# Image 2's sorted products by half steps, and its adding gathers without free steps

## The chip, the cores and the metric

The kernel runs on one core of a Trainium2 chip. The metric is the device time of one launch in microseconds (us). The engines of the core run programs of their own and wait for each other by semaphores: TensorE (PE: matmuls and transposes), ScalarE (ACT: activations, evictions of PSUM), VectorE (DVE: elementwise work and reductions), GpSimd (POOL: here powers, and the issue of indirect DMAs) and SyncE (SP: issues DMAs). ACT issues a few DMAs too.

## The reference

Two layers on four images x of 32 channels and 128 x 128 pixels, all in float32:

```python
# layer 0: attention over the 4096 pixels of each image, by 2 x 2 pixel groups as 128 channels
energy = einsum('bci,bcj->bij', q, q);  d = sqrt(diagonal(energy))
attn = softmax(energy / (d[:, :, None] * d[:, None, :]))
out = gamma * einsum('bcj,bij->bci', q, attn) + xs
# layer 1, on the result as tokens t of 128 features
t = t + L1_attn(layernorm(t), Wk, Wq, Wv)      # linear attention, 8 heads
t = t + L1_ffn(layernorm(t), router_w, ...)    # top 2 of 8 experts per token
```

The expert part computes `softmax(x @ router_w + router_b)`, takes the two largest of eight probabilities per token, scales them to a sum of one, and adds the two experts' products with these weights.

## The kernel before

**Layer 0** (`attend`). An image's 4096 pixels are 8 chunks of 512. The matrix of energies is symmetric, so only chunk pairs (i, jc) with jc up to i are computed, in blocks of 128 x 512. A *step* does one block: PE computes `pe` (L551), ACT takes its exp with a row sum (L554), PE multiplies the block of two steps before into `po` (L440), VectorE transposes it in groups (L369), SP moves groups through DRAM and back (L473 and L488), and some five steps later PE multiplies the mirrored block into `pg` (L375), while ACT sums it once more (`junk`, L380). An image takes 144 steps; the last one (image 3) takes 152, since in its last chunk row two blocks are computed a second time the other way round (`pe_back`, L529 and L532).

**Layer 1** (`layer1`) follows an image's attention. `close_rows(kc)`, kc = 0 to 3, finishes eight row groups: it divides by the sums (L704), adds (L726), takes statistics (L729) and their power on POOL (`rsa`, L164 called from L632, then `nba`, L633), normalises on ACT (L639; for kc = 2 and 3 of the last image half of it on VectorE, L739) and adds the Gram matrix on PE (L671). `close_rows` waits until the transposed shares that its rows need have been added. Then come the small matrices, the linear attention, and the router.

The experts of images 0 to 2 work on sorted tokens, by two halves h of an image (`sorted_experts`, L915). 32 *scatters* of POOL (L994) write the normalised tokens to DRAM in the order of their expert. Then a loop (L1070) goes over 39 tiles of 128 sorted tokens, as 20 pairs: it loads pair `at` (L1022, on SP), evicts what the step before left in PSUM (`done()`: ACT copies transposed tiles, L1032; VectorE scales products by the token's weight, L1038; SP stores them to DRAM, L1042), and issues on PE the products of pair `at - 4` (L1056) and the transposes of pair `at - 3` (L1063). So a pair's transposes are evicted one iteration later and are the weights of the matmuls after that. At last 32 *adding gathers* of POOL (L1107) bring each token's two results back from DRAM and add them to the token in `acc`. They go by groups of eight; ACT fetches the group's tokens first (L1092), and SP stores the finished group to the output (L1098). Image 3's experts are done without sorting, in `last_parts`.

**What sets the order.** For PE, VectorE, ACT and SP the program order is the order of issue (`manual_schedule`, L1315), and POOL's powers, first scatters and gathers are pinned too. The order comes from generators: each `yield` ends one advance. `attend` yields before and after each step, and the main loop (L1333 to L1349) moves the streams at both places, so a step moves a stream of layer 1 by two advances; `idle(n)` is 2n yields, that is n steps. Image 2's stream therefore runs along image 3's attention. Within a stream the parts run side by side (`stagger`, L166). Each scatter and gather waits for the last exp that was issued before it, "not more of these at a time than steps have". A half's gathers begin when its loop has ended and the other half's scatters (for h = 0) or gathers (for h = 1) are issued. What is left of the streams when image 3's attention ends is issued at once (L1357 to L1359: the drain), in the order of the images, before `last_parts`.

The variable `rate` (L1101) is the number of gathers between two yields: 1 for images 0 and 1, 2 for image 2, whose groups moreover had one free step after each four gathers.

Of the kernel before, what the change touches and what calls it, by code (L numbers as in the profile page):

```python
# [22 lines left out]
def kernel(  # L23
# [45 lines left out]
    B, C, H, W = x.shape  # L69
# [59 lines left out]
    def wait_for(inst, others, why):  # L129
        for other in others:  # L130
            tc.add_manual_dep(
                inst, other.name, mybir.DependencyInfo(mybir.DependencyClass.Sync, mybir.DependencyReason.DATA),
                reason=why,
            )
# [24 lines left out]
    def pinned(inst):  # L159
        tc.keep_in_program_order(inst)  # L160
        return inst
# [16 lines left out]
    def idle(n):  # L178
        for _ in range(2 * n):
            yield  # L180
# [416 lines left out]
    def layer1(b, st):  # L597
# [276 lines left out]
        def attention_rows(u):  # L874
# [32 lines left out]
            if u % 2:  # L907
                for _ in route(u // 2):
                    yield
                    yield  # L910
                yield
                yield
                yield from sorted_experts(u // 2)

        def sorted_experts(h):  # L915
# [66 lines left out]
            def offset(ap):  # L982
                return bass.IndirectOffsetOnAxis(ap=ap, axis=0)
# [4 lines left out]
            for n in range(2 * HR):  # L988
# [19 lines left out]
                if n % 4 == 3 and (b < B - 2 or n % 8 == 7):  # L1008
                    yield from idle(1)
            turns[h].append("moved")  # L1010
            xs_made[h][:], xs_read[h][:] = scatters, []
            yield from idle(3)

# [7 lines left out]
            def load(g, n):  # L1021
                inst = nc.sync.dma_start(bufs[g % 6][:, :n], rows_of(xs[h], g, n))  # L1022
                wait_for(inst.ins, xs_made[h], "a tile holds tokens of any row")
                xs_read[h].append(inst.ins)
# [45 lines left out]
            for at in range(len(pairs) + 5):  # L1070
                if at < len(pairs):
                    load(*pairs[at])
                if done:
                    done()
                yield
                turned, applied = (pairs[at - d] if 0 <= at - d < len(pairs) else None for d in (3, 4))
                done = products(turned, applied) if turned or applied else None
                yield
# [11 lines left out]
            def fetch(g):  # L1090
                accs[g] = work.tile([P, 4, D], F32, tag="acc", name=f"acc_{b}_{g}", bufs=3)
                nc.scalar.dma_start(accs[g], t2[:, ts(g, 4)])  # L1092

            def put(g):
                for r1 in range(2):
                    for s in range(2):
                        p0 = s * 64 + r1 * 32
                        nc.sync.dma_start(dst_out[s, r1, :, ts(g, 4), :], accs[g][p0 : p0 + 32])  # L1098

            groups = list(range(r0 // 4, (r0 + HR) // 4))  # L1100
            rate = 1 if b < B - 2 else 2  # L1101
            fetch(groups[0])
            yield from idle(2)
            for g in groups:
                for n in range(8):
                    i, k = n // 4, 4 * g + n % 4
                    inst = nc.gpsimd.indirect_dma_start(  # L1107
                        accs[g][:, n % 4, :], None, ys, offset(place[:, i, k : k + 1]), compute_op=ALU.add
                    )
                    wait_for(pinned(inst).ins, exps, "not more of these at a time than steps have")  # L1110
                    if (n + 1) % rate == 0:
                        yield
                        yield
                    if rate == 2 and n % 4 == 3:
                        yield from idle(1)
                    if n == 3 and g != groups[0]:
                        put(g - 1)
                    if n == 3 and g != groups[-1]:
                        fetch(g + 1)
# [280 lines left out]
```

## Time and profile before

| | us |
|---|---|
| median of the runs (3) | 1706.38 |
| lowest to highest | 1706.34 to 1708.11 |
| the profiled execution | 1708.0 |
| its span, first to last instruction | 1706.2 |
| mean granted clock of TensorE | 0.989 |

| engine | busy us | share of the span |
|---|---|---|
| PE | 1645.4 | 96% |
| ACT | 927.5 | 54% |
| VectorE | 880.4 | 52% |
| POOL | 630.9 | 37% |

The profile is of one execution. A row of a timeline gives start, duration, engine, line of the code, operation, what is written and read, how often, and in brackets how long the engine sat idle before and what ended that. The chain of waits goes back from the last instruction, at each point to what released it. Busy PE is modelled, so full PE is not PE at its peak. Image 3's attention runs from about 1156 to 1566 us; `last_parts` ends the kernel.

### The profile page before, as it was taken

The numbers are of one execution on the slowest core, as the hardware profiler recorded it, in microseconds if no ns is written. First come the engines' busy times: TensorE is split into PE (matmuls) and PEld (weight loads), VectorE is DVE, ScalarE is ACT, GpSimd is POOL, SyncE is SP. The second block draws the span as 40 slices with busy tenths as digits, with TensorE's granted clock in tenths as the row PEclk, the third lists the DMA queues.
The fourth block names the chain that finished last, engine by engine and source line by source line (L and its number), as shares of the span: only waits on it lengthen the run. The fifth ranks groups of instructions, "written<-read, shape, count | busy, mean of one in ns | idle before, by whom it ended". The sixth has DMA issues, their size and how long they took to land.

```text
span 1706.2 us, 21751 instructions
## 1 busy us (share of the span) xinstructions
PE 1645.4 (96%) x5458; PEld 876.4 (51%) x5458; DVE 880.4 (52%) x2251; ACT 927.5 (54%) x2893; POOL 630.9 (37%) x565
## 2 busy tenths in 40 slices
PE   8999999999999999999999999999999999999288
PEld 5444544455554455555554455555554455546243
DVE  4433334467485334377477334357568333346187
ACT  3555445466565555556575555556565555555076
POOL 1000000011024432454554532455555640567666
PEclk9999999999999999999999999999999999999699
DMA  4554756754458687985678676895578867993201
GB/s 133 169 178 155 208 177 212 254 178 162 164 162 261 209 248 214 250 229 148 185 216 255 229 223 215 249 251 159 166 210 240 260 213 229 236 248 63 44 12 39
DMA packets 248555, 326.53 MB, mean 191 GB/s; under 512 B 31472, under 2 KB 180080, under 8 KB 234096
## 3 DMA queue, kind: packets, MB, share of 16 engines
q1 hardware_dynamic: 206416, 285.62, 52.9%
q0 software_dynamic: 33792, 25.58, 8.5%
q10 hardware_dynamic: 8224, 13.93, 2.7%
q8 instruction: 46, 0.75, 0.2%
q14 instruction: 77, 0.63, 0.1%
HBM read 154.49 MB, written 175.80 MB: 194 GB/s over the span
## 4 chain that ended last, share of the span: by engine, by line
PE 81%; DVE 7%; ACT 4%; POOL 3%; DMA 2%; issue 2%; SPq 1%; ACTq 0%; DVEq 0%; POOLq 0%
PE po L440 23%; PE pe L551 22%; PE pg L375 19%; PE pys L1056 3%; PE py L1192 2%; PE pg L396 2%; POOL acc L1107 2%; PE pys L1063 1%; ACT xn L639 1%; PE pgram L671 1%; PE pat L797 1%; DVE df L704 1%; PE ptq L313 1%; ACT pr L554 1%; DVE F L369 1%
## 5 line engine op out<-in xcount | busy, mean ns | idle before, releaser
L554 ACT ACTIVATE pr<-pe 128x512 f32<-128x512 f32 (+1 forms) x576 | 322.3, 560 | 517.0 <-PE pe L551 429.9
L440 PE MATMUL po<-pr,qT 128*128 128x512 f32 (+3 forms) x1152 | 549.8, 559 | 3.9 <-ACT o L445 2.7
L551 PE MATMUL pe<-qn,qn 128*128 128x512 f32 x896 | 458.9, 594 | 2.0 <-ACT pr L554 1.7
L375 PE MATMUL pg<-F,qT 128*128 128x512 f32 x880 | 449.6, 592 | 0.8 <-DVE F L369 0.6
L1107 POOL DMA_INDIRECT acc<-ys,place x192 | 301.9, 1572 | 304.7 <-ACT pr L554 198.3
L369 DVE STREAM_TRANSPOSE F<-pr 128x512 f32<-128x512 f32 x440 | 306.4, 702 | 165.7 <-ACT pr L554 129.9
L440 PEld LDWEIGHTS po<-pr,qT 128*128 128x128 f32 x1152 | 214.8, 190 | 250.7 <-issue 222.2
L380 ACT ACTIVATE junk<-F 128x512 bf16<-128x512 f32 x440 | 272.8, 620 | 1.0 <-DMA F<-blocks 1.0
L375 PEld LDWEIGHTS pg<-F,qT 128*128 128x128 f32 x880 | 166.8, 190 | 195.2 <-issue 179.0
L994 POOL DMA_INDIRECT xs<-xn,place x192 | 185.6, 967 | 196.7 <-ACT pr L554 123.6
L551 PEld LDWEIGHTS pe<-qn,qn 128*128 128x128 f32 x896 | 152.6, 191 | 100.5 <-issue 93.3
L385 DVE TENSOR_TENSOR o<-o,pg 128x512 f32<-128x512 f32 x110 | 75.5, 686 | 214.3 <-PE pg L375 207.2
L1038 DVE TENSOR_TENSOR results<-pys,xn 128x256 f32<-128x256 f32 x120 | 50.1, 417 | 190.6 <-ACT xn L1032 151.7
L164 POOL TENSOR_TENSOR rn<-ss,neg_half 128x8 f32<-128x8 f32 (+1 forms) x17 | 26.9, 1582 | 321.2 <-DVE ss L325 321.2
L554 ACT ACTIVATION_READ_ACCUMULATOR pr<-pe 128x1 f32 x576 | 111.9, 194 | 0.0
L1032 ACT ACTIVATE xn<-pys 128x256 f32<-128x256 f32 x120 | 45.2, 377 | 114.9 <-PE pys L1063 95.7
L1056 PEld LDWEIGHTS pys<-ew_sb,xn 128*128 128x128 f32 x468 | 70.0, 191 | 48.4 <-issue 46.8
L551 PE MATMUL pe<-qn 128*128 128x512 f32 (+3 forms) x256 | 90.2, 435 | 0.7 <-ACT qn L344 0.7
L380 ACT ACTIVATION_READ_ACCUMULATOR junk<-F 128x1 f32 x440 | 84.4, 192 | 0.0
L639 ACT ACTIVATE xn<-T,nba,rsa 128x128 f32<-128x128 f32 x120 | 49.2, 483 | 43.5 <-POOL nba L633 43.5
L1056 PE MATMUL pys<-ew_sb,xn 128*128 x468 | 71.6, 275 | 0.0
L164 POOL TENSOR_TENSOR rsa<-dm_a,neg_half 128x8 f32<-128x8 f32 x16 | 30.1, 1881 | 112.0 <-DVE sv_a L631 111.7
(211 smaller groups left out, 1506.5 us busy)
## 6 DMA issues: line engine op xcount, KB each, us to landing
blocks<-F SPq DMA_DIRECT2D x110, 1024.0 KB
F<-blocks SPq DMA_DIRECT2D x220, 192.0 KB
F<-blocks SPq DMA_DIRECT2D x220, 128.0 KB
xn<-xs SPq DMA_DIRECT2D x114, 132.0 KB
ys<-results SPq DMA_DIRECT2D x114, 128.0 KB
F<-blocks SPq DMA_DIRECT2D x220, 64.0 KB
below<-F SPq DMA_DIRECT2D x31, 384.0 KB
out_dram<-acc SPq DMA_DIRECT2D x128, 64.0 KB
```

The costliest lines, as they stand in the source:

```text
L164: pinned(nc.gpsimd.tensor_tensor(dst, src, neg_half.to_broadcast(list(src.shape)), ALU.pow))
L369: f()
L375: nc.tensor.matmul(pg.rearrange("p (a f) -> p a f", a=4), st["qT"][i][:, ib, :], G[:, :, ib], start=(ib == 0), stop=(ib == NJ - 1),)
L380: nc.scalar.activation(junk, G[:, :, ib], AF.Copy, accum_out=st["sums"][:, NJ * i + ib, jc : jc + 1])
L385: nc.vector.tensor_tensor(o, o, pg.rearrange("p (a j c) -> p a j c", a=4, c=S), ALU.add)
L440: nc.tensor.matmul(row["po"][:, lo:hi], qT[blk // NJ][:, blk % NJ, :], w, start=start, stop=(row["left"] == 0))
L551: nc.tensor.matmul(pe[:, c0:], qn[jc][:, ts(j, P)], qn[i][:, c0:], start=True, stop=True)
L554: nc.scalar.activation(pr[:, c0:], pe[:, c0:], AF.Exp, accum_out=sums[:, t, i : i + 1]).ins
L639: nc.scalar.activation(xn[:, k, :D], T[:, k, :], AF.Identity, scale=rs[:, k, :], bias=nb[:, k, :])
L994: inst = nc.gpsimd.indirect_dma_start(xs[h], offset(place[:, i, k : k + 1]), xn[:, k, :], None)
L1056: nc.tensor.matmul(p[:, 2 * P + j * D : 2 * P + j * D + D], bufs[6 + g % 2][:, j, :D], weights[:, bass.ds(begins[2 * (g % 2) + j], D)], st ...
L1107: inst = nc.gpsimd.indirect_dma_start(accs[g][:, n % 4, :], None, ys, offset(place[:, i, k : k + 1]), compute_op=ALU.add)
```

## The change

It concerns image 2 (`b == B - 2`) alone and has two parts. In the loop of `sorted_experts` the yield between the evictions and the products goes, so that an iteration takes one advance, half a step, where it took two. And among the adding gathers the free step after each four goes, so that two are issued with every step. Loads, stores, products, evictions, gathers and their number stay as they are, and so do images 0, 1 and 3.

```diff
@@ -1008,6 +1008,7 @@
                 if n % 4 == 3 and (b < B - 2 or n % 8 == 7):
                     yield from idle(1)
             turns[h].append("moved")
+            hurried = b == B - 2
             xs_made[h][:], xs_read[h][:] = scatters, []
             yield from idle(3)
 
@@ -1072,7 +1073,8 @@
                     load(*pairs[at])
                 if done:
                     done()
-                yield
+                if not hurried:
+                    yield
                 turned, applied = (pairs[at - d] if 0 <= at - d < len(pairs) else None for d in (3, 4))
                 done = products(turned, applied) if turned or applied else None
                 yield
@@ -1111,8 +1113,6 @@
                     if (n + 1) % rate == 0:
                         yield
                         yield
-                    if rate == 2 and n % 4 == 3:
-                        yield from idle(1)
                     if n == 3 and g != groups[0]:
                         put(g - 1)
                     if n == 3 and g != groups[-1]:
```

## The prediction

> **What bounds the kernel now.** I read the page first, then the chain of waits of the last 170 us, then timelines by engine and the busy times by stretch. Times below are microseconds from the span's start.
>
> ```profile
> span 1706.2 us, 21751 instructions
> PE 1645.4 (96%) x5458; PEld 876.4 (51%) x5458; DVE 880.4 (52%) x2251; ACT 927.5 (54%) x2893; POOL 630.9 (37%) x565
> PE 81%; DVE 7%; ACT 4%; POOL 3%; DMA 2%; issue 2%; SPq 1%; ACTq 0%; DVEq 0%; POOLq 0%
> ```
>
> TensorE sets the time nearly everywhere. The busy times by stretch (length, then PE, PE loads, DVE, ACT, POOL busy with counts, granted clock, DMA share, GB/s) show where it doesn't:
>
> ```profile
> 1460.00:1500.00 40.00, 40.00 (x153) 22.89 (x152) 15.58 (x29) 21.34 (x65) 23.69 (x17) 1.00 0.95 241
> 1580.00:1609.00 29.00, 0.00 (x0) 0.00 (x0) 0.00 (x0) 0.00 (x0) 24.64 (x17) 0.57 0.38 54
> ```
>
> From 1580 to 1609 only GpSimd (POOL) works. The timelines of VectorE, POOL and ScalarE (ACT) say on what (start, duration, engine, line, operation; in brackets the idle time before and what ended it):
>
> ```profile
> 1578.90 0.17 DVE L631 TENSOR_SCALAR sv_a<-sv_a 128x8 f32<-128x8 f32 x1
> ...
> 1605.45 1.54 POOL L1107 DMA_INDIRECT acc<-ys,place  x1 [0.30 <-issue]
> 1606.43 2.27 POOL L164 TENSOR_TENSOR rsa<-dm_a,neg_half 128x8 f32<-128x8 f32 x1
> 1608.78 0.20 POOL L633 TENSOR_TENSOR nba<-sv_a,rsa 128x8 f32<-128x8 f32 x1
> 1609.02 1.65 ACT L639 ACTIVATE xn<-T,nba,rsa 128x128 f32<-128x128 f32 x4 [33.27 <-POOL nba L633]
> ```
>
> The chain of waits goes the same way, from these gathers to rsa, nba, ACT and then PE:
>
> ```profile
> 1606.99 1.72 POOL rsa L164
> ...
> 1609.02 0.50 ACT xn L639
> ...
> 1609.57 3.79 PE pgram L671 x16
> ```
>
> Image 3's last row statistics (kc = 3) are ready at 1579.07, but their power (rsa) stands on POOL behind image 2's last 18 gathers, which the program put there when the stream was drained. Free of them, nba would be done at 1579.07 + 0.04 + 1.67 + 0.08 + 0.20 = 1581.0 (1.67 is rsa alone, at 1567.11) instead of 1608.98. The prize is **28.0 us**.
>
> [...]
>
> **Where the change puts things.** I count image 3's attention steps 1 to 152 (one exp of L554 or L532 each). Nearly every step moves image 2's stream by two advances, one yield each, one before and one after the step; between one step's second advance and the next step's first no attention work is issued. That order matters below.
>
> Half 0's sorted products (L1070 to L1080) take 25 yields instead of 50, from step 79. Its gathers also need half 1's scatters, which end in step 99 as before; fetch and idle(2) put the first gather in step 102 instead of 110. A group of 8 gathers takes 4 steps instead of 6 (the removed idle(1) comes twice a group). So half 0 gathers in steps 102 to 119, half 1 in 122 to 138 (before: 139 and on, 18 left for the drain). All are issued 14 steps before attention ends. The 28.0 us go, and with them the cold clock after the idle: the 16 matmuls of pgram took 3.79 us against 2.40 at 1568.88, and the first pgv some 0.3 more: **1.7 us**.
>
> **Cost 1: two products back to back.** Before, a step with a pair takes 3.24 us, without 2.58 (exps at 1501.56, 1504.80; 1510.73, 1513.30): a product costs 0.66, PE never waiting. The number of products is unchanged, so these 0.66 only move. But a product's matmuls need the tile that ScalarE evicted from the product before (L1032), and now two products often stand next to each other:
>
> ```profile
> 1503.52 0.38 PE L1063 MATMUL pys<-ident,xn 128*128 128x128 f32 x2
> 1503.94 0.38 ACT L1032 ACTIVATE xn<-pys 128x256 f32<-128x256 f32 x1 [1.08 <-PE pys L1063]
> 1504.35 0.42 DVE L1038 TENSOR_TENSOR results<-pys,xn 128x256 f32<-128x256 f32 x1 [2.73 <-ACT xn L1032]
> ```
>
> From the start of the last transpose (1503.63) to the eviction 0.31, eviction 0.38, to the next matmul 0.05 (ACT ends 1574.41, PE goes on 1574.46), less the 0.11 at which they follow anyway: 0.63. [...] between 0 and 0.25 I take 0.1: 0.73. Counting the yields along the steps, 8 products of each half are such a second one: 16 x 0.73 = 11.7. The other 24 follow a step, but their eviction now stands on ACT behind that step's exp and junk: exp start + 0.58 + 0.62 + 0.38 + 0.05 = 1.63, where the product's matmul came at 1.51 and its weight load at 1.09. Between 0 and 0.5 I take 0.22: 5.3. **Sum 17** (13 to 21). PE is the bound there (40.00 of 40.00 busy), so nothing hides it.
>
> **Cost 2: gathers now queue before an earlier rsa.** Back to back a gather takes 1.84:
>
> ```profile
> 1505.75 1.54 POOL L1107 DMA_INDIRECT acc<-ys,place  x1 [2.43 <-ACT pr L554]
> 1507.60 1.54 POOL L1107 DMA_INDIRECT acc<-ys,place  x1 [0.30 <-issue]
> 1509.44 1.54 POOL L1107 DMA_INDIRECT acc<-ys,place  x1 [0.30 <-ACT junk L380]
> ```
>
> Two a step are 3.68 us against 2.58 of a step without products. Half 0's gathers lie mostly beside half 1's products (2.58 + 2 x 0.66 + 0.95 = 4.85 us a step) and POOL keeps up; half 1's don't. Image 3's first rows (kc = 0) issue their rsa in step 137, unchanged (it waits for the transposed shares, not for "sorted"), now behind 30 gathers. From step 122's exp (1487.30 before): 0.95 to the first gather, 29 x 1.84 + 1.54 = 54.9, 2.03 from the last gather to ACT's normalise (1606.99 to 1609.02), 1.64 for it, 0.27 for pgram's last row: 59.8. PE gets past that pgram (L671, after step 140) at 1539.32 - 1487.30 = 52.0, less 4 for six products no longer there: 48.0.
>
> ```profile
> 1535.54 1.64 ACT L639 ACTIVATE xn<-T,nba,rsa 128x128 f32<-128x128 f32 x4
> 1537.08 0.58 ACT L554 ACTIVATE pr<-pe 128x512 f32<-128x512 f32 x1
> 1538.43 1.05 PE L671 MATMUL pgram<-xn 128*128 128x128 f32 x8
> ```
>
> Behind the waiting normalise stand exps of steps 140 and on; behind pgram all PE. **11.8 us** (10 to 14). After that PE's clock is halved as at 1609; there 0.11 of 31 us were lost, 3.4, of which 0.7 in a dip from 1638.7 on: **2.6 us** (1 to 4).
>
> **What is moved at no or little cost.** Each pair's load and store (SP, 132 and 128 KB) come twice a step, 4 issues of 0.42; with the block moves 2.5 us of SP in 4.85. A load follows the store of two products before; two steps and five products later its transposes come, at the least 2 x 2.58 + 4.4 x 0.66 + 3 x 0.73 + 2 x 0.22 = 10.7 us, against 1.4 to evict and issue and the 2.7 to 5.9 that transfers in the chain of waits took to land. DMA: 241 GB/s x 3.24 us is 781 KB a step; 260 and 43 KB for the gathers more make 1084 KB in 4.85 us, 224 GB/s, no denser than now. Stores of gathered groups (L1098) stand on SP before image 3's last block moves, and wait for late gathers: group 5's are landed 32 us after step 122's exp, the move of step 134 is then at 34 instead of 32; its shares come after the pgram stall, which covers 2 us. ACT's fetches reuse a buffer stored 4 steps before. For all this **1 us** (0 to 4); without its cover a late load stops PE one for one.
>
> **Sum against the profiled execution** (1708.0, its span 1706.2, 1.8 outside): -28.0 - 1.7 + 17 + 11.8 + 2.6 + 1 = +2.7, so 1710.7. The median of the runs is 1.6 lower: 1709.1.
>
> **Rivals.** *A, the above*: the 28 us are handed back, 1709 (own range 1702 to 1718). *B, faster*: TensorE waits less than I think between two adjacent products, at L1056 after L1032. For it speaks that the modelled matmul ends are no measurement; against, ACT's 0.38 alone times 16 is 6. If all adjacent products cost 4 together: -29.7 + 4 + 15.4 = -10, 1696. The sign turns where they cost 14.3 in all, and 0.2% is reached below 11. *C, slower*: loads land late. SP is in order; a burst of six block moves takes 2.8 us, and a semaphore shared with an ACT fetch held SP up to 5.4 (its wait list). Some 6 bursts in the doubled loops at 2 us each: 12 more, 1721. Against: 10.7 - 1.4 - 5.9 leaves 3.4 us to spare after the slowest landing. *D, it does not do what it says*: half 0's gathers still wait for late stores and part of the drain stays, with Cost 1 paid: 1720. Against: the stores end in step 93.
>
> **Chances.** A 0.55, B 0.20, C 0.18, D 0.07. No change within 0.2% (3.4 us) is about what measurement tells. A gives 0.05 faster, 0.22 same, 0.28 slower; B 0.16 and 0.04; C and D slower: 0.21, 0.26, 0.53. Range 1695 to 1721: it leaves out the far halves of B, C and D.
>
> **What would show it.** Right: no POOL gather after some 1575; kc = 3's rsa starts at DVE's end; steps of 4.5 to 5 us with PE idle before L1056; a PE idle of 10 to 14 us before the first pgram of image 3, with ACT L639 waiting for nba, and the clock at half after it. Wrong: PE busy throughout the doubled loops (B), PE waiting at L1063 for DMA (C), or gathers up to kc = 3's rsa (D).

## The result, and the profile after

| | before | after |
|---|---|---|
| median of 7 runs each, us | 1706.38 | 1713.20 |
| lowest to highest | 1705.69 to 1708.40 | 1711.24 to 1715.61 |
| ratio, 95% interval | | 1.0038 (1.0026 to 1.0049) |
| profiled execution, its span | 1708.0, 1706.2 | 1711.8, 1710.0 |

The changed kernel is slower by 0.38%. Between the profiled executions the difference is 3.8 us, between the medians 6.8: the profiled one of before lay 1.6 over its median, that of after 1.4 under. What follows accounts for the 3.8. In the changed file L1032, L1056, L1063 and L1107 are L1033, L1057, L1064 and L1109.

The page of after, its head and its engines:

```profile
span 1710.0 us, 21761 instructions
...
PE 1654.2 (97%) x5458; PEld 874.0 (51%) x5458; DVE 878.9 (51%) x2251; ACT 926.2 (54%) x2893; POOL 628.7 (37%) x565
```

PE is busy 8.8 us more with the same 5458 instructions. Busy times of after by stretch (length, then PE, PE loads, DVE, ACT, POOL busy with counts, clock, DMA share, GB/s):

```profile
1382.00:1420.00 38.00, 33.09 (x136) 18.14 (x135) 12.37 (x25) 16.22 (x50) 10.65 (x12) 1.00 0.61 180
1449.00:1497.00 48.00, 42.49 (x176) 23.94 (x175) 15.00 (x34) 20.05 (x64) 30.66 (x20) 1.00 1.02 254
...
1555.00:1572.00 17.00, 5.21 (x15) 2.59 (x14) 0.00 (x0) 2.79 (x9) 14.29 (x11) 0.77 0.45 76
```

The first two stretches lie in half 0's and half 1's products, where PE now idles 4.91 and 5.51 us; the third is a new stall, in which POOL alone works. The waits of after, TensorE's (waited for in all, times, longest), name both:

```profile
PE pgram L671 <- ACT xn L639: 13.9, 4, 11.8
PE pys L1057 <- ACT xn L1033: 10.2, 17, 1.3
```

**The products.** Two adjacent ones in the timeline of after:

```profile
1400.84 0.38 PE L1064 MATMUL pys<-ident,xn 128*128 128x128 f32 x2
1401.31 0.38 ACT L1033 ACTIVATE xn<-pys 128x256 f32<-128x256 f32 x1 [1.08 <-PE pys L1064]
...
1401.75 0.52 PEld L1057 LDWEIGHTS pys<-ew_sb,xn 128*128 128x128 f32 x4 [0.77 <-ACT xn L1033]
1401.75 0.71 PE L1057 MATMUL pys<-ew_sb,xn 128*128 x4 [0.53 <-ACT xn L1033]
```

The transposes, their eviction by ACT and the next product's matmuls follow one after the other. A doubled step takes 4.91 us (exps at 1403.58 and 1408.49) where 2.58 + 2 x 0.66 would be 3.90. The exp of step 130 comes 20.5 us later than before.

**The gathers.** POOL's timeline of after around the stall and at the end of attention:

```profile
1566.82 1.54 POOL L1109 DMA_INDIRECT acc<-ys,place  x1 [0.30 <-issue]
1567.81 2.26 POOL L164 TENSOR_TENSOR rsa<-dm_a,neg_half 128x8 f32<-128x8 f32 x1
1570.15 0.20 POOL L633 TENSOR_TENSOR nba<-sv_a,rsa 128x8 f32<-128x8 f32 x1
...
1613.26 1.63 POOL L164 TENSOR_TENSOR rsa<-dm_a,neg_half 128x8 f32<-128x8 f32 x1 [9.96 <-DVE sv_a L631]
```

The last row is kc = 3's power: it starts as VectorE ends, no gather before it. The second is kc = 0's: it ends a row of 30 gathers begun at 1512.90, and ACT and PE stood behind it (ACT's and PE's timelines of after):

```profile
1570.39 1.65 ACT L639 ACTIVATE xn<-T,nba,rsa 128x128 f32<-128x128 f32 x4 [14.21 <-POOL nba L633]
```

```profile
1570.93 2.08 PE L671 MATMUL pgram<-xn 128*128 128x128 f32 x8 [11.79 <-ACT xn L639]
```

The clock was recorded at half from 1564.17 to 1574.41, and these 8 matmuls took 2.08 us, where the next 8 took 1.05. From the exp of step 139 to that of step 142 another 13.7 us are lost (14.3 by step 140, of which 0.6 come back). So: -28.0 (kc = 3's power no longer queued) + 20.5 + 13.7 - 2.4 (warm clock at the end: the 16 matmuls of pgram 2.07 us in place of 3.79, the first pgv 2.10 in place of 2.59, the rest small) = +3.8.

### The profile page after: what moved, and what is told of

It is laid out like the page before. It is cut to its first block, busy times and chain, and to the rows that moved or that the text cites. A ratio compares the mean times of both kernels' runs of the same rounds, so it can differ in the third digit from the quotient of the medians.

```text
span 1710.0 us, 21761 instructions
## 1 busy us (share of the span) xinstructions
PE 1654.2 (97%) x5458; PEld 874.0 (51%) x5458; DVE 878.9 (51%) x2251; ACT 926.2 (54%) x2893; POOL 628.7 (37%) x565
## 5 line engine op out<-in xcount | busy, mean ns | idle before, releaser
L440 PE MATMUL po<-pr,qT 128*128 128x512 f32 (+3 forms) x1152 | 549.6, 559 | 3.9 <-ACT o L445 2.0
L551 PE MATMUL pe<-qn,qn 128*128 128x512 f32 x896 | 458.7, 594 | 2.0 <-ACT pr L554 1.7
L1109 POOL DMA_INDIRECT acc<-ys,place x192 | 300.2, 1564 | 265.7 <-ACT pr L554 193.7
L440 PEld LDWEIGHTS po<-pr,qT 128*128 128x128 f32 x1152 | 214.7, 190 | 251.5 <-issue 224.4
L551 PEld LDWEIGHTS pe<-qn,qn 128*128 128x128 f32 x896 | 153.7, 191 | 107.4 <-issue 99.9
L1057 PEld LDWEIGHTS pys<-ew_sb,xn 128*128 128x128 f32 x468 | 67.0, 191 | 63.6 <-issue 32.9
L1033 ACT ACTIVATE xn<-pys 128x256 f32<-128x256 f32 x120 | 45.1, 376 | 96.7 <-PE pys L1064 83.8
L551 PE MATMUL pe<-qn 128*128 128x512 f32 (+3 forms) x256 | 91.0, 438 | 0.7 <-ACT qn L344 0.7
L1057 PE MATMUL pys<-ew_sb,xn 128*128 x468 | 75.5, 283 | 11.8 <-ACT xn L1033 10.2
L1192 PE MATMUL py<-ew_sb,xn 128*128 128x512 f32 x128 | 61.3, 621 | 5.3 <-ACT tmp L1149 4.1
```

What stands on the lines that cost most here:

```text
L440: nc.tensor.matmul(row["po"][:, lo:hi], qT[blk // NJ][:, blk % NJ, :], w, start=start, stop=(row["left"] == 0))
L551: nc.tensor.matmul(pe[:, c0:], qn[jc][:, ts(j, P)], qn[i][:, c0:], start=True, stop=True)
L1057: nc.tensor.matmul(p[:, 2 * P + j * D : 2 * P + j * D + D], bufs[6 + g % 2][:, j, :D], weights[:, bass.ds(begins[2 * (g % 2) + j], D)], st ...
L1109: inst = nc.gpsimd.indirect_dma_start(accs[g][:, n % 4, :], None, ys, offset(place[:, i, k : k + 1]), compute_op=ALU.add)
L1192: nc.tensor.matmul(bank, xn[:, k, :D], ew_sb[:, 4 * h : 4 * h + 4, :], start=True, stop=True)
```

## The experiments

Theory T: the products lose their time in the round trip from PE to ACT and back between adjacent products; the second loss is the queue of gathers ahead of kc = 0's power. Its rivals: R1, the products' loops lose their time to the transfers, twice as many a step; R2, the gathers are the whole loss; R3, the stall is of something else than the gathers; R4, at twice the pace the transfers are the limit wherever the products stand; R5, half 1's gathers must start by step 122 to be out of the way; R6, after the attention POOL has room for the gathers, so that the order in the drain alone gives the 28 us. *Delay* is how much later than before the exp of step 130 comes, less the offset that step 78 had already; *stall* what is lost from there to step 142; *left* the gathers that POOL starts after the last exp; *power* is the start of kc = 3's power.

| kernel | delay | stall | left | power | median us | ratio to before (95%) |
|---|---|---|---|---|---|---|
| before | | | 20 | 1606.43 | 1706 to 1708 | |
| after | 20.6 | 13.7 | 0 | 1613.26 | 1713.20 | 1.0038 (1.0026 to 1.0049) |
| half steps alone | 20.5 | 0 | 9 | 1607.04 | 1707.06 | 1.0000 (0.9991 to 1.0008) |
| gathers alone | 0.7 | 7.1 | 5 | 1597.42 | 1695.96 | 0.9932 (0.9915 to 0.9948) |
| tile used later | 14.4 | 14.6 | 0 | 1609.15 | 1707.50 | 1.0000 (0.9991 to 1.0009) |
| free steps in half 1 | 20.3 | 0 | 0 | 1600.64 | 1698.02 | 0.9943 (0.9926 to 0.9959) |
| transposes ahead | 17.4 | 14.6 | 0 | 1610.98 | 1712.90 | 1.0041 (1.0026 to 1.0056) |
| the two above together | 19.5 | 0 | 0 | 1598.85 | 1697.69 | 0.9945 (0.9931 to 0.9959) |
| half steps in half 1 | 10.0 | 1.5 | 10 | 1600.20 | 1700.25 | 0.9957 (0.9943 to 0.9971) |
| in half 1's last ten iterations | 10.4 | 0 | 9 | 1596.63 | 1696.36 | 0.9937 (0.9924 to 0.9951) |
| before, power first | 0 | 0 | 20 | 1579.46 | 1696.30 | 0.9935 (0.9921 to 0.9948) |
| last ten, power first | 11.4 | 0 | 9 | 1593.19 | 1689.96 | 0.9896 (0.9881 to 0.9911) |

**Each part of the change alone.** The first keeps the free steps among the gathers, the second keeps the whole steps of the products. Against the changed kernel:

```diff
+                    if rate == 2 and n % 4 == 3:
+                        yield from idle(1)
```

```diff
-                if not hurried:
-                    yield
+                yield
```

> Half steps alone: image 2's products take half a step per pair as in the changed kernel, the gathers keep the free step after each four. Theory T (TensorE waits for the eviction between two adjacent products; the gathers' queue is the second loss): the exp of step 130 comes 20.5 us (18 to 23) after that of before, as in the changed kernel. Half 1's gathers then go in steps 128 to 151, some 10 of them ahead of the power of kc = 0, at POOL's pace: TensorE's idle time before image 3's first pgram is under 4 us (11.8 in the changed kernel). About 8 gathers are left when attention ends, kc = 3's nba comes at about 1607 (1608.98 before), in all 1704 (1700 to 1709). Rival R2 (the products cost nothing worth naming, the whole loss is that of the gathers on POOL): the exp of step 130 comes less than 5 us late, and the time is about 1690.

> Gathers without free steps alone, the products stay at a step per pair. T: no delay in the products' loops (exp of step 130 within 1.5 us of before). Half 0's gathers end some 8 steps earlier, half 1's go in steps 133 to 151. Some 8 gathers stand ahead of kc = 0's power: TensorE idles 0 to 4 us before image 3's first pgram. POOL falls some 10 us behind by the end of attention, so kc = 3's nba comes at 1590 to 1595 (1608.98 before): 1690 (1685 to 1696). R2 (the gathers back to back are the whole loss): slower than before, 1712 or more.

The 20.5 us go with the half steps and the stall with the gathers: R2 falls. POOL's timeline with half steps alone shows why the first brings nothing: kc = 0's power finds a short queue, but kc = 3's has the rest of the gathers ahead of it.

```profile
1552.56 1.54 POOL L1109 DMA_INDIRECT acc<-ys,place  x1 [0.30 <-issue]
1553.93 1.88 POOL L164 TENSOR_TENSOR rsa<-dm_a,neg_half 128x8 f32<-128x8 f32 x1
...
1606.04 1.54 POOL L1109 DMA_INDIRECT acc<-ys,place  x1 [0.30 <-issue]
1607.04 2.26 POOL L164 TENSOR_TENSOR rsa<-dm_a,neg_half 128x8 f32<-128x8 f32 x1
```

With the gathers alone the time fell by 11 us, not by the 16 expected: kc = 0's power came at 1541.36, still behind back-to-back gathers, and so did kc = 1's and 2's later. PE waited 4.5, 3.1 and 5.1 us for the three. POOL's timeline and TensorE's wait list of that kernel:

```profile
1540.37 1.54 POOL L1107 DMA_INDIRECT acc<-ys,place  x1 [0.30 <-issue]
1541.36 2.26 POOL L164 TENSOR_TENSOR rsa<-dm_a,neg_half 128x8 f32<-128x8 f32 x1
```

```profile
PE pgram L671 <- ACT xn L639: 15.0, 7, 5.1
```

**The round trip taken away.** A product uses the tile turned two iterations before.

```diff
-            for at in range(len(pairs) + 5):
+            for at in range(len(pairs) + 5 + hurried):
+                if done:
+                    done()
                 if at < len(pairs):
                     load(*pairs[at])
-                if done:
-                    done()
...
-                turned, applied = (pairs[at - d] if 0 <= at - d < len(pairs) else None for d in (3, 4))
+                gaps = (3, 5) if hurried else (3, 4)
+                turned, applied = (pairs[at - d] if 0 <= at - d < len(pairs) else None for d in gaps)
```

> The changed kernel, but a product uses the tile transposed two iterations before, not the one before (pair at - 5 in place of at - 4, the loop one iteration longer), so that one more product stands between a tile's eviction and the matmul that reads it. Loads, stores, their number and their place per half step are the same. T: the waits of L1057 for the eviction are gone (under 3 us in all, 11.8 + some of the loads' in the changed kernel), the doubled step takes 3.9 to 4.1 us in place of 4.91, the exp of step 130 comes under 4 us later than before in place of 20.5; the queue ahead of kc = 0's power stays and costs as much or a little more, 13.7 to 18: 1693 to 1697 in all. Rival R1 (the loops lose their time to the transfers and SP's issues, twice as many a step): the doubled step stays at 4.7 to 4.9 us, and the time at 1710 to 1714.

TensorE's timeline of this kernel in half 0, and its wait list:

```profile
1399.32 0.61 PE L1057 MATMUL pys<-ew_sb,xn 128*128 x4
1399.76 0.38 PE L1064 MATMUL pys<-ident,xn 128*128 128x128 f32 x2
1399.98 0.61 PE L1057 MATMUL pys<-ew_sb,xn 128*128 x4
1400.43 0.38 PE L1064 MATMUL pys<-ident,xn 128*128 128x128 f32 x2
1400.65 1.02 PE L551 MATMUL pe<-qn,qn 128*128 128x512 f32 x2
```

```profile
PE pgram L671 <- ACT xn L639: 14.4, 4, 12.2
PE pys L1064 <- DMA xn<-xs: 8.9, 7, 2.5
```

In the step shown PE goes through two products without a gap, the doubled step takes 3.91 us (exps at 1397.80 and 1401.71), and at step 104, past half 0's products, the delay is 2.5 us in place of 11.6. So the round trip is the cause of that half's loss, as T has it. In half 1 no product waited for an eviction either, but there, with denser transfers (in the changed kernel 254 GB/s, where half 0 had 180), the loss came back as waits for loads, 8.5 us of PE in five of them; after two of these the clock was recorded at half for 3.41 us each (behind the one of 2.33 us that ended at 1456.73, the next two matmuls of L440 took 1.70 us, where two took 1.02 in half 0). The waits may in part be of this edit's making: a buffer is free later in it, so a load is issued after the evictions, and on SP behind a store. For half 1 the cause therefore rests on the same waits in the trace of after, not on an edit that removed the loss. T's time was missed by 10 us for this. R1 is wrong for the changed kernel, where PE waited for a load once, 0.086 us; but once the round trip is gone, late loads are what comes next.

**The queue taken away.** The changed kernel with the free step after each four gathers kept in half 1:

```diff
+                    if rate == 2 and h == 1 and n % 4 == 3:
+                        yield from idle(1)
```

> The changed kernel, with the free step after each four gathers kept in half 1 alone (half 0's follow each other). T: Cost 1 stays (exp of step 130 20.5 us late). Half 1's 32 gathers go in steps 122 to 145, at 4 a 3 steps (7.4 us of POOL in 7.8 us), so POOL hardly falls behind: TensorE idles under 2 us before image 3's first pgram, its clock is not halved there, and no gather is left when attention ends (kc = 3's power starts as VectorE ends). Time: after - 13.7 = 1699.5 (1697 to 1703). R3 (TensorE's stall there is of something else than the gathers issued ahead, the transposed shares say): the stall stays at 10 us or more and the time at 1711 or more.

POOL's timeline: kc = 0's power and kc = 3's both wait for VectorE, not for gathers.

```profile
1551.91 1.54 POOL L1109 DMA_INDIRECT acc<-ys,place  x1 [0.30 <-issue]
1555.00 1.67 POOL L164 TENSOR_TENSOR rsa<-dm_a,neg_half 128x8 f32<-128x8 f32 x1 [1.55 <-DVE sv_a L631]
...
1600.64 1.63 POOL L164 TENSOR_TENSOR rsa<-dm_a,neg_half 128x8 f32<-128x8 f32 x1 [9.97 <-DVE sv_a L631]
```

The stall is gone, the products' delay stays, the time is 15 us under the changed kernel's: R3 falls.

**The transposes ahead**, alone and with those free steps. In `products` the loop of L1064 moves ahead of the matmuls of L1057 (they stand at L1049 and L1061 then):

```diff
+                if turned:
+                    g, n = turned
+                    for j in range(n):
+                        nc.tensor.transpose(p[:, ts(j, P)], bufs[g % 6][:, j, :D], ident)
                 if applied:
                     g, n = applied
...
-                if turned:
-                    g, n = turned
-                    for j in range(n):
-                        nc.tensor.transpose(p[:, ts(j, P)], bufs[g % 6][:, j, :D], ident)
```

> The changed kernel with the two parts of a product exchanged on TensorE: the transposes of pair at - 3 go ahead of the matmuls of pair at - 4. Loads and stores stay where they are. Between a tile's transposes and the matmuls that read it then stand the matmuls of the pair before and the transposes of the pair after, 0.66 us in place of nothing. Theory T: the wait of two adjacent products for the eviction goes, the steady doubled step takes 3.9 us in place of 4.91, and TensorE waits for the eviction of a product under 3 us in all. A load has as much lead in half steps as in the changed kernel, but the half steps are shorter (1.95 us in place of 2.46), so T leaves room for 0 to 5 us of waits for loads in half 1. The exp of step 130 comes 3 to 9 us later than before (20.5 in the changed kernel), the queue of gathers stays (13.7 to 15): 1698 (1694 to 1703). Rival R4 (at twice the pace the transfers are the limit, wherever the products stand, as the first such kernel's half 1 suggests): 8 us or more of waits for loads in half 1, step 130 12 us late or more, 1704 to 1708.

> The kernel with the transposes ahead, and the free step after each four gathers kept in half 1. T: both costs gone, the gain of the drain kept: no stall over 2 us before image 3's first pgram, no gather left at the end of attention; 13.7 to 15 under the kernel with the transposes ahead alone, 1684 (1679 to 1690), faster than before by 1.0 to 1.6%. R4: as the kernel with free steps in half 1 alone less what the transfers leave, 1690 to 1694.

The timeline of the first of them:

```profile
1398.22 0.38 PE L1049 MATMUL pys<-ident,xn 128*128 128x128 f32 x2
...
1398.44 0.61 PE L1061 MATMUL pys<-ew_sb,xn 128*128 x4
...
1398.88 0.38 PE L1049 MATMUL pys<-ident,xn 128*128 128x128 f32 x2
1399.14 0.38 ACT L1033 ACTIVATE xn<-pys 128x256 f32<-128x256 f32 x1 [0.87 <-PE pys L1061]
...
1399.58 0.71 PE L1061 MATMUL pys<-ew_sb,xn 128*128 x4 [0.32 <-issue]
```

Both expectations failed. The transposes end at 1398.60, but the eviction starts at 1399.14: it waited for the product's last matmul (L1061, its end modelled at 1399.05), which lies in the same PSUM tile. Only the second product's transposes (0.22 us of PE) came to stand in the gap, the idle time fell from 0.53 to 0.32, the doubled step from 4.91 to 4.49, the delay by 3 us. This agrees with T's mechanism, but the edit did not take it away. R4 falls as well: it needed 8 us or more of waits for loads in half 1, and they were 1.1. With the free steps in half 1 the same edit gave 1697.69 us, where those free steps alone gave 1698.02.

**Fewer half steps.** With the free steps of half 1's gathers, and half steps only in half 1, or only in its last ten iterations:

```diff
-            hurried = b == B - 2
+            hurried = b == B - 2 and h == 1
```

and for the second also

```diff
-                if not hurried:
+                if not hurried or at < 15:
```

> Half steps for half 1's products alone (half 0's take a whole step per pair as before), half 0's gathers without free steps, half 1's with them. Theory T: the loss of adjacent products is halved with the number of them: the exp of step 130 comes 10.3 us (9 to 12) after that of before, where both halves gave 20.5. Half 0's gathers go in steps 110 to 126, half 1's from 128 to 151, none or two are left at the end of attention; no stall over 2 us before image 3's first pgram. So 1706.4 - 30.4 (the drain and its cold clock) + 10.3 = 1686 (1682 to 1690). Rival R5 (half 1's gathers must start by step 122 to be out of the way): several are left at the end, 1.84 us each, kc = 3's power waits for them, 1690 to 1697.

> As the kernel with half steps in half 1 alone, but only the last ten of its 25 iterations take half a step; its gathers start in the same step, since half 0's end no sooner. T: the loss goes by the number of adjacent products: 4 us (3 to 6) at step 130 in place of 10.3, all else the same, 1680 (1676 to 1685). R5: 1684 to 1692.

With one half the delay is 10.0 us: half the products, half the loss. The last ten iterations cost as much, 10.4, where T had 3 to 6. PE's wait list of that kernel has a part of it:

```profile
PE pys L1064 <- DMA xn<-xs: 3.9, 2, 2.6
```

Two waits for loads make 3.9 us. After the first the clock was recorded at half for 3.41 us (1483.64 to 1487.05), in which the transposes, L551 and L440 took about 1.5 us more from start to start than at full clock. PE waited for evictions five times here, and at the 1.01 us of a doubled step in the changed kernel these are about 5. So the count of adjacent products holds as an estimate; late loads and the clock, which T left out, are the rest. R5 was right on the gathers, though both times lay over its ranges too. I had placed them by the yields, 110 to 126 and from 128; POOL started the last of half 0 in step 133 and 129, and 10 and 9 were left at the end. 64 gathers at 1.84 us are 118 us of POOL; from step 110 (1454) to kc = 3's statistics (1579 without delay) there are 125, into which four powers and every pause must fit as well.

**The order in the drain.** Image 3's stream is drained before image 2's, in the kernel before and in the one with half steps in the last ten iterations:

```diff
-    for steps, _ in steady:
+    for steps, _ in reversed(steady):
```

> The kernel before, with image 3's stream drained ahead of image 2's, so that the power of kc = 3 stands on POOL before the 18 left gathers instead of behind them; nothing else differs. Theory T (POOL is a queue, and the prize is where the gathers stand in it): kc = 3's nba comes at 1581 in place of 1608.98. The 18 gathers, 33 us of POOL, then run from 1581 to 1614.5, and the next power on POOL (rsf of the attention's norm, which would be due at 1594.5 to 1596) waits for them until 1614 in place of its 1623.78: 9 to 10 us are kept, 1697 (1694 to 1700). Rival R6 (after the attention POOL has room enough, and the 28 us are free to take by the order alone): 1677 to 1681.

> The kernel with half steps in the last ten iterations of half 1, with image 3's stream drained ahead of image 2's as well. There 8 gathers (14.8 us of POOL) stood ahead of kc = 3's power, of which 5.4 us on the path. T: kc = 3's nba at 1593.2 in place of 1598.96 and its 16 matmuls of pgram at 2.1 us in place of 3.64: 7 us gained; rsf then due at 1606 waits for the last of the 8 gathers until 1608: 1691.5 (1689 to 1694). R6: 1689.

POOL's timelines, first of the kernel before with this edit, then of the other:

```profile
1579.46 1.67 POOL L164 TENSOR_TENSOR rsa<-dm_a,neg_half 128x8 f32<-128x8 f32 x1 [6.02 <-DVE sv_a L631]
1581.20 0.20 POOL L633 TENSOR_TENSOR nba<-sv_a,rsa 128x8 f32<-128x8 f32 x1
...
1613.52 1.55 POOL L1107 DMA_INDIRECT acc<-ys,place  x1 [0.30 <-issue]
1614.50 2.27 POOL L164 TENSOR_TENSOR rsf<-dm_f,neg_half 128x8 f32<-128x8 f32 x1
```

```profile
1593.19 1.64 POOL L164 TENSOR_TENSOR rsa<-dm_a,neg_half 128x8 f32<-128x8 f32 x1 [10.42 <-DVE sv_a L631]
...
1608.73 1.54 POOL L1109 DMA_INDIRECT acc<-ys,place  x1 [0.30 <-DVE T L1213]
1609.72 2.25 POOL L164 TENSOR_TENSOR rsf<-dm_f,neg_half 128x8 f32<-128x8 f32 x1
```

The power comes 27 us earlier without a single half step, and the time falls by 11: the next power, rsf, now stands behind the same gathers (1614.50, before 1623.78). R6 falls. In the other kernel only 8 gathers are left to stand before rsf, and it is the fastest of all, 1689.96 us, 1.04% (0.89 to 1.19) under the kernel before. T's 1691.5 and R6's 1689 lie too close for that run to tell them apart.

## Why the prediction was right, and where a term was off

The case that it held likeliest came: the gain of the drain handed back in two places. By its steps:

- **The prize, 28.0, and 1.7 for the cold clock.** Right: kc = 3's power starts at VectorE's end, the warm clock gave 2.4. Half 0's first gather came in step 102 and half 1's in step 122, as forecast, and none was left.
- **Cost 1, 17 (13 to 21).** Mechanism right, size at the upper end: 20.5. A second product of a pair costs about 0.80 (1.01 a doubled step less 0.21 for the first; a step with a single product took 3.45 us, which is 2.58 + 0.66 + 0.21) where 0.73 stood (0.63 from the timeline, and 0.1 that was the author's guess): 12.8 for 16. The products after a step at 0.22 were right after a full step, 16 x 0.21 = 3.4, and wrong after two shorter ones, where PE reaches the product sooner and the eviction still stands behind two other passes of ACT: after a step with L440 of 128x256, and after one with L440 of 128x128 and no mirrored share, PE waited 0.37 and 1.32 us, once each a half, 3.4 in all. About 1 us of the 20.5 is not attributed. Of these losses PE's idle time shows 11.8 only; the others lie in its longer busy time (L1057's four matmuls 0.71 us where they took 0.61 without the wait).
- **Cost 2, 11.8, and 2.6 for the clock.** Right: 13.7 together against 14.4. PE idled 11.79 us, behind 30 gathers, as counted. The 0.11 that the forecast took is from the granted clock of 0.89 over 1609 to 1640 in the kernel before; in its first 5.76 us, up to 1614.76, that clock was 0.50.
- **The moved loads and stores, 1.** Nothing to be seen; the 3.4 us to spare were enough. Experiments that shortened the spare time or broke the even pace had such waits: 8.9 us with the tile used later, 3.9 and 3.7 in the two kernels with half steps in the last ten iterations.
- **The sum, +2.7.** The profiled executions differ by 3.8. The forecast of 1709.1 lies 4.1 us under the median all the same: 1.1 is Cost 1's miss less the other terms', 3.0 that the two profiled executions stand differently to their medians. Why is open. That the sign came right is in part luck: the sum is what is left of gains of 29.7 and costs of 32.4, and with Cost 1 at the low end of its range, 13, it would have been -1.3.

Rivals: B needed the adjacent products under 14.3 us; they cost 20.5. C's late loads and D's left gathers did not come in the changed kernel.

## What to carry to other kernels

Before two pieces of work of one stream are put next to each other on the engine that sets the time, look for what they pass through another engine: the attention step between them had been hiding a round trip (0.53 us of idle PE in the doubled step of after), and the new cost times the count is to be set against the gain. POOL took its work in the order of issue: in the kernel before, kc = 3's power waited 27.4 us (1579.07 to 1606.43) with its inputs ready. Such a queue was full or not by its own pace, not by the places of issue (half 0's last gather, issued for step 126 with half steps in half 1, started in step 133): count its whole work (64 x 1.84 us) against the stretch that it must fit into, and ask of each urgent instruction in it, not only of the one that you free, what stands ahead. Where the gain is that one short instruction no longer waits, try first to issue it earlier; the remaining queue then falls on the next one (in the kernel before with its drain turned round, on rsf: at 1614.50, behind 18 gathers).

## What the runs showed of the hardware that was not expected

- With the transposes ahead, the eviction of their half of a PSUM tile started 0.54 us after their modelled end, with the end of the matmuls into the other half (modelled at 1399.05, the eviction at 1399.14). Whether the engine or the program's semaphores ask for that, these runs don't tell apart.
- The clock in the stall of after was recorded at half 5.0 us after PE's last work (1559.14 to 1564.17) and full again 3.5 us after its first (1570.93 to 1574.41). In the kernel before it went to half 4.1 us after PE's last work (1579.96 to 1584.04) and was full again 5.2 us after its first (1609.57 to 1614.76). These stretches lasted 10.24 and 30.72 us, and each kernel had one of 3.41 later (from 1642.67 in after, from 1638.66 in before): three, nine and one times 3.41. So in both stalls the half clock lasted on into the work that followed. With half steps in the last ten iterations it began at 1483.64, 2.3 us into a wait of 2.62, sooner than in the two long stalls.
- A gather took 1.54 us and 0.30 to the next with 54 GB/s of traffic in all (the drain of before) and with 254 (the products' stretch of after) alike. So the traffic made no difference to its pace between these two; what sets the pace was not tried apart.
